# Gate and up products in float32r from exact 12-bit parts, and row additions by accumulating transfers, in a cross-attention and fp4 SwiGLU layer

## The chip, the cores and the metric

The kernel is written in Bass and Tile and runs on one core of a Trainium2 chip. The metric is the device time of one execution in microseconds (us). A core has four compute engines with one in-order instruction queue each, TensorE (PE), VectorE (DVE), ScalarE (ACT) and GpSimd (POOL), a fifth queue, SyncE (SP), that here issues nearly all transfers, 16 DMA engines that carry them out, the on-chip memory SBUF, and PSUM, where TensorE writes its results, in 8 banks of 128 x 512 float32 values.

## The reference

`x` is 8 batches x 512 rows x 256 columns in float32, the context 8 x 64 x 256. Cut to what matters, with `ln` for a layernorm without gamma and beta:

```python
y  = ln(x)
y  = ln(y + attention(y, y, y, causal=True)) * g1 + beta1
y  = ln(y + attention(y, ctx, ctx)) * g2 + beta2
ff = relu(y @ w1 + b1) @ w2 + b2              # 256 -> 1024 -> 256
x  = x + ln(y + ff) * g3 + beta3
q  = fp4(ln(x))                               # blocks of 16 values
h  = silu(q @ fp4(w_gate).T) * (q @ fp4(w_up).T)   # 256 -> 704
x  = x + fp4(h) @ fp4(w_down).T               # 704 -> 256
```

Attention has one head and no projections. `fp4` divides each block of 16 values by a sixth of its largest magnitude, rounds to the grid 0, 0.5, 1, 1.5, 2, 3, 4, 6 with the sign, and multiplies back.

## The kernel before

**Tiles.** Each batch is 4 row tiles (`NT`) of 128 rows (`P`). The width 256 is `ND` = 2 chunks of 128, the MLP's 1024 is `NF` = 8, the 704 (`I`) of gate and up is `NI` = 6 chunks, the last one 64 wide, and two halves (`HI`) of 352. Per batch there are five stages: self-attention (0), cross-attention (1), MLP (2), the gate/up products with silu (3) and the down product (4).

**Line numbers of the stages.** Transposes by TensorE stand at L419, the squares of a norm (ACT) at L488, its sums at L480 and L496, its power -1/2 on POOL at L503. `scaled_norm` has two VectorE steps per row tile, (r - mean) * g at L537 and r * rstd + beta at L545. `by_row` adds a row vector to four row tiles on VectorE (L557); it adds b2 to `r` and beta3 to `x`. `fp4` is L578 to L610: a reduction, two small steps on 44 block scales, three `scalar_tensor_tensor` or `tensor_tensor` steps of 704 columns with an Abs on ACT (L597) between them, and a last product (L610). Self-attention has its scores at L767, exp at L778 and values at L800. `turned` transposes either by products of TensorE, evicted by ACT (L831), or by transfers: ACT splits the values into planes of 16 bits (L843), SP's queue writes them to DRAM and reads them back transposed. Cross-attention is L883 (scores, laid into 128 rows of 256), L896 (ACT copies them out of PSUM), L900 (transposes), L927 (values). The MLP is L961 (first product), L969 (relu by ACT with b1 as bias), L981 (second product), L992 (VectorE adds it to `r`), L1003 and L1011 (norm and sum with `x`).

**Gate, up and down.** `zT` is the quantized, transposed input of the batch; `wgu` holds both quantized weights. For each row tile and each half of 352 columns, two float32 products (L1036), gate and up, go into a bank each. ACT takes silu of the gate bank into `h` (L1048), VectorE multiplies by the up bank (L1055). `h` is quantized, turned (planes by ACT at L1071 and two transfers, in the last batch by TensorE), multiplied by `wd` (L1116), added to `x` by VectorE (L1126) and stored by SP (L1133). A float32 product runs as two matmul instructions, so the 256 gate/up products are 512 instructions in the trace.

```python
plan.op("PE", ND * pe(HI), product, reads=[zT, ready["wgu"]], writes=[pair[j]],
        takes=[*pair, h])
```

**The order.** Nothing runs where the source puts it. Every step is a `plan.op`: engine, estimated cost, buffers read and written. `Plan.order` then lists all steps: each engine takes, of the steps whose inputs are there by the estimates and whose buffers are free, the one with the smallest key, the latest time at which it could start if the stages are to end at the times in `DUE` (a row for each batch, a column for each stage; `push` is added to the keys of the weights' steps). Steps are issued in that order, and each engine's queue keeps it on the chip. Buffers come in kinds with a fixed number (`x` 6, `z` 8, `hT` 8, `wide` 8 for `h` and its quantized magnitudes, and so on); buffers of an ordered kind can only be taken in the order in which the source creates them. At the head, the weights `w_gate`, `w_up` and `w_down` are quantized and turned by transfers into `wgu` and `wd`, beside the first batches.

Of the kernel before, what the change touches and what calls it, by code (L numbers as in the profile page):

```python
# [12 lines left out]
U16 = mybir.dt.uint16  # L13
AF = mybir.ActivationFunctionType
# [5 lines left out]
P = 128  # L20
# [11 lines left out]

PE_PASS = 0.429 / 512
# [5 lines left out]
TURN = 2.6  # L39
# [4 lines left out]
LOAD_EARLY = 2191.0  # L44
DUE = [
    [-1877.0, 638.0, 1236.0, -86.0, 359.0],
    [-498.0, 1140.0, 299.0, -53.0, 352.0],
    [251.0, 920.0, -109.0, 452.0, 665.0],
    [2244.0, 599.0, -92.0, 754.0, 95.0],
    [1032.0, 759.0, 1302.0, 1127.0, 22.0],  # L50
    [818.0, -579.0, 119.0, -1108.0, 586.0],
    [771.0, -1583.0, 341.0, 621.0, 85.0],
    [127.0, -388.0, -430.0, -94.0, -1479.0],
    [-2334.0],
# [6 lines left out]

def dve(cols):
    return 0.06 + cols * 1.06e-3
# [197 lines left out]
def kernel(  # L261
# [43 lines left out]
    def several(name, count, shape):  # L305
        return [fixed(f"{name}_{k}", shape) for k in range(count)]
# [3 lines left out]
    plan.kind("x", several("x", 6, [P, NT, D]))  # L310
# [3 lines left out]
    z_homes = several("z", 8, [P, D + 2])  # L314
    plan.kind("y0", y0_homes)
    plan.kind("z", z_homes)
    plan.kind("zT", several("zT", 6, [P, ND, SZ]))
# [3 lines left out]
    plan.share("zqT", "turned", 3)  # L321
    plan.kind("e", several("e", 1, [P, NT * (NT + 1) // 2 * P]))
    plan.kind("r", several("r", 3, [P, NT, D]))
    plan.kind("kq", several("kq", 4, [P, S // 2]))
    plan.kind("xp", several("xp", 6, [P, NT, SZ]))
    plan.kind("xpT", several("xpT", 3, [P, NT // 2 * P]))
# [3 lines left out]
    plan.kind("wide", several("h", 8, [P, NI * P]), ordered=False)  # L330
    plan.share("h", "wide", 5)
    plan.share("hm", "wide", 3)
    plan.share("wq", "wide", 7)
# [57 lines left out]
    c_rows = fixed("c_rows", [NF, P])  # L391
    b1_sb = fixed("cols", [P, NF])

    vecs = {}
    for name, v in (
        ("g1", g1), ("beta1", beta1), ("g2", g2), ("beta2", beta2), ("b2", b2),
        ("g3", g3), ("beta3", beta3),
    ):
        vecs[name] = (fixed(f"v_{name}", [P, D]), v)
    w1_sb = fixed("w1", [P, ND, DFF])  # L400
    w2_sb = fixed("w2", [P, NF, D])
    wgu = fixed("wgu", [P, ND, 2 * I])
    wd = fixed("wd", [P, NI, D])

    plan.kind("const", ["const"] * 13, ordered=False)
    ready = {}
    for name in ("cols", "g1", "beta1", "g2", "g3", "beta2", "beta3", "b2", "w1", "w2", "wgu", "wd", "pads"):
        ready[name] = plan.buf("const")
# [16 lines left out]
    def norm_stats(v, view, pairs):  # L425
# [18 lines left out]
        for ts_ in pairs:  # L444
            lo, hi = ts_[0], ts_[-1] + 1
            for t in ts_:
                plan.op(
                    "DVE", 0.33, lambda t=t: nc.vector.bn_stats(st(t), view(t)),
                    reads=[(v, t)], writes=[(s, ("st", t))],
                )  # L450
            plan.op(
                "DVE", 0.1 + 0.09 * len(ts_), lambda ts_=ts_: variances(ts_),
                reads=[(s, ("st", t)) for t in ts_],
                writes=[(s, ("var", lo))] + [(s, t) for t in ts_],
            )
            plan.op(
                "POOL", 1.05,
                lambda lo=lo, hi=hi: nc.gpsimd.tensor_tensor(
                    s.ap[:, 36 + lo : 36 + hi], s.ap[:, 32 + lo : 32 + hi], mhalf[:, lo:hi], ALU.pow
                ),  # L460
                reads=[(s, ("var", lo))], writes=[(s, ("rstd", t)) for t in ts_],
            )
            plan.op(
                "DVE", 0.15,
                lambda lo=lo, hi=hi: nc.vector.scalar_tensor_tensor(
                    s.ap[:, 40 + lo : 40 + hi],
                    s.ap[:, 24:32].rearrange("p (t k) -> p t k", k=2)[:, lo:hi, 0],
                    -1.0, s.ap[:, 36 + lo : 36 + hi], ALU.mult, ALU.mult,
                ),
                reads=[(s, ("rstd", t)) for t in ts_] + [(s, t) for t in ts_],  # L470
                writes=[(s, ("shift", t)) for t in ts_],
            )
        return s

    def sums_stats(v, view, s):
# [9 lines left out]
        for t in range(NT):  # L485
            plan.op(
                "ACT", 0.52,
# [43 lines left out]
    def scaled_norm(r, s, g, beta):  # L531

        sums_stats(r, lambda t: r.ap[:, t, :], s)
        for t in range(NT):
# [9 lines left out]
                "DVE", 0.4,  # L544
                lambda t=t: nc.vector.scalar_tensor_tensor(  # L545
                    r.ap[:, t, :], r.ap[:, t, :], s.ap[:, 36 + t : 37 + t], vecs[beta][0],
                    ALU.mult, ALU.add,
                ),
                reads=[(s, ("rstd", t)), ready[beta]], writes=[(r, t)],
            )  # L550

    def by_row(v, vec, f):

        for t in range(NT):
            plan.op(
                "DVE", dve(D),
                lambda t=t: nc.vector.tensor_tensor(  # L557
                    v.ap[:, t, :], v.ap[:, t, :], vecs[vec][0], f
                ),
                reads=[(v, t), ready[vec]], writes=[(v, t)],  # L560
            )
# [7 lines left out]
    def fp4(v, view, mkind, nblk):  # L569
# [18 lines left out]
        plan.op("DVE", 0.7, scales, reads=[q], writes=[q])  # L588
# [34 lines left out]

    def weights():
# [3 lines left out]
        plan.batch = 0  # L628
        for j, w in enumerate((w_gate, w_up)):
            for half, groups in enumerate(((0, 1), (2, 3, 4))):  # L630
# [23 lines left out]
                def apart(v=v, m=m, n=n, wide=wide):  # L654
                    k = halves(v.ap[:, :wide], D)
                    nc.scalar.copy(planes_of(m.ap[:, :wide], D), k)
                    if n > wide:
# [9 lines left out]
                )  # L667
                plan.op(
                    "SP", 1.8,
                    lambda d=d, g=g, j=j, groups=groups: nc.sync.dma_start_transpose(  # L670
                        wgu[:, :, ds(j * I + groups[0] * P, g * P)].bitcast(U16),
                        d.ap[:g].rearrange("g p h k -> (g p h) k"),
                    ),
                    reads=[d], writes=[(ready["wgu"], (j, half))], lag=TURN,
                )
                if not half:
# [9 lines left out]
                    def rest(d=d, j=j):  # L686
                        for c in range(ND):
                            nc.sync.dma_start_transpose(
                                wgu[:, c, ds(j * I + WI * P, RI)].bitcast(U16),
# [3 lines left out]
                    plan.op(  # L693
                        "SP", 1.2, rest, reads=[d], writes=[(ready["wgu"], (j, "rest"))], lag=TURN
                    )
# [28 lines left out]
    def columns():  # L724
        plan.batch = -1
        pt = plan.buf("bank")

        plan.op(
            "SP", 0.65, lambda: nc.sync.dma_start(c_rows, b1.rearrange("(c p) -> c p", p=P)),
            writes=[ready["cols"]],  # L730
        )
        plan.op(
            "PE", 0.2, lambda: nc.tensor.transpose(pt.ap[:, :NF], c_rows, ident[:NF, :NF]),
# [3 lines left out]
            "ACT", 0.2, lambda: nc.scalar.copy(b1_sb, pt.ap[:, :NF]),  # L737
            reads=[pt], writes=[ready["cols"]],
        )
        for name in ("g1", "beta1", "g2", "beta2", "b2", "g3", "beta3"):  # L740
# [4 lines left out]
            )  # L745

    def self_attention(b, xs):
# [13 lines left out]
        for k in range(NT):  # L761
# [3 lines left out]
            def scores(k=k, n=n, sc=sc):  # L765
# [11 lines left out]
                "ACT", act(n, True),  # L777
# [42 lines left out]
        scaled_norm(r, s, "g1", "beta1")  # L820
# [39 lines left out]
    def cross_attention(b, r, zs):  # L860
# [11 lines left out]
        )  # L872
        yT = turned(r, "yT", b < BY_PRODUCTS[1], lambda t: r.ap[:, t, :])
# [6 lines left out]
        def products():  # L880
            for c in range(ND):
                for i in range(2):
# [3 lines left out]
                    )  # L886

# [6 lines left out]
        plan.op("PE", 1.05, products, reads=[yT, zT], writes=[keys])  # L894
        kq = plan.buf("kq")
        plan.op("ACT", act(S // 2), lambda: nc.scalar.copy(kq.ap, keys.ap[:, : S // 2]), reads=[keys], writes=[kq])  # L896
# [48 lines left out]
        scaled_norm(r, s, "g2", "beta2")  # L945

    def mlp(b, r, xs):
# [5 lines left out]
        by_row(r, "b2", ALU.add)  # L953
        by_row(xs, "beta3", ALU.add)
        hT = []
        for f in range(NF):
            hp, h = plan.buf("bank"), plan.buf("hT")

            def product(f=f, hp=hp):
# [8 lines left out]
                "ACT", act(S, True),  # L968
# [3 lines left out]
                reads=[hp, ready["cols"]], writes=[h],  # L972
# [3 lines left out]
        for t in range(NT):  # L976
            fp = plan.buf("bank")

            def product(t=t, fp=fp):
# [11 lines left out]
                "DVE", 0.42,  # L991
# [27 lines left out]
    def glu(b, xs, s):  # L1019
# [7 lines left out]

        def gate_up(t):
            plan.stage = 3
            h = plan.buf("h")  # L1030
            for n in range(2):
                pair = [plan.buf("bank") for _ in range(2)]
                for j in range(2):
                    def product(t=t, n=n, j=j, gp=pair[j]):
                        for c in range(ND):
                            nc.tensor.matmul(  # L1036
                                gp.ap[:, :HI], zT.ap[:, c, ts(t, P)],
                                wgu[:, c, ds(j * I + n * HI, HI)],
                                start=(c == 0), stop=(c == ND - 1),
                            )  # L1040

                    plan.op(
                        "PE", ND * pe(HI), product, reads=[zT, ready["wgu"]], writes=[pair[j]],
                        takes=[*pair, h],
# [3 lines left out]
                    lambda n=n, h=h, gp=pair[0]: nc.scalar.activation(  # L1048
                        h.ap[:, ts(n, HI)], gp.ap[:, :HI], AF.Silu
                    ),  # L1050
                    reads=[pair[0]], writes=[(h, n)], table="silu",
                )
                plan.op(
                    "DVE", 0.45,
                    lambda n=n, h=h, gp=pair[1]: nc.vector.tensor_tensor(  # L1055
                        h.ap[:, ts(n, HI)], h.ap[:, ts(n, HI)], gp.ap[:, :HI], ALU.mult
                    ),
                    reads=[pair[1]], writes=[(h, n)],
# [52 lines left out]
        def last(t, hqT):  # L1111
            op = plan.buf("bank")

            def product(hqT=hqT, op=op):
                for c in range(NI):
# [8 lines left out]
            plan.op(  # L1124
                "DVE", 0.42,
                lambda t=t, op=op: nc.vector.tensor_tensor(  # L1126
                    xs.ap[:, t, :], op.ap[:, :D], xs.ap[:, t, :], ALU.add
                ),
                reads=[op], writes=[(xs, t)],
            )  # L1130
# [6 lines left out]

        if b == B - 1:
            hs = [gate_up(t) for t in range(NT)]
            for t in range(NT):  # L1140
                down(t, hs[t])
        else:
            for t in range(NT):
                down(t, gate_up(t))
# [18 lines left out]
    plan.push = 2035.0  # L1163
# [41 lines left out]
```

## Time and profile before

| | before |
|---|---|
| median of 3 runs (lowest to highest) | 575.76 us (575.72 to 576.1) |
| span of the profiled execution | 574.5 us |
| time of the profiled execution | its span; the runs' times lie 1.2 to 1.6 us above it |
| PE busy | 563.8 us, 98% |
| DVE busy | 447.8 us, 78% |
| ACT busy | 361.8 us, 63% |
| POOL busy | 62.2 us, 11% |
| gate/up products, L1036 | 512 instructions, 27% of the chain |
| down products, L1116 | 384 instructions, 15% of the chain |
| bytes moved by DMA | 66.88 MB, mean 116 GB/s |

The page is that of one execution, taken by the hardware profiler. "Busy" is the time in which an engine ran an instruction; "chain" is the chain of work that ended last, followed back from the last instruction, with its shares by engine and line. Groups of instructions are written line, engine, operation, output<-inputs, tile shape, count. The granted TensorE clock was full (1.000) through the whole span. Column names of a stage table are: start and end of the stage, its length, then busy time (instructions) of PE, PEld (the weight loads), DVE, ACT and POOL, mean granted clock, DMA share and GB/s.

### The profile page before, as it was taken

How to read it: one execution, taken by the hardware profiler on the slowest of the kernel's cores; microseconds unless marked ns; L12 is line 12 of the kernel's file. 1: busy time of each engine (PE TensorE's matmuls, PEld its weight loads, DVE VectorE, ACT ScalarE, POOL GpSimd, SP SyncE). 2: the span in 40 equal slices, each digit the busy share in tenths (PEclk: the TensorE clock that was granted, in tenths of full speed). 3: DMA queues.
4: the chain of work that ended last, by engine and by line, in shares of the span. 5: the costliest groups of instructions: out<-in, count | busy, mean ns of one | idle time of the engine just before them, and what ended most of it. 6: DMA issues, size and time to landing. Idle time of an engine off the chain costs nothing.

```text
span 574.5 us, 7037 instructions
## 1 busy us (share of the span) xinstructions
PE 563.8 (98%) x2209; PEld 391.2 (68%) x2209; DVE 447.8 (78%) x1125; ACT 361.8 (63%) x761; POOL 62.2 (11%) x93
## 2 busy tenths in 40 slices
PE   5999999999999999999999999999999999999997
PEld 2767584866747668658486667766765866877686
DVE  4789988869998865755259999978997656399892
ACT  4677869598887672791638558887845256364431
POOL 3521101011200120110101102210100000010000
PEclk9999999999999999999999999999999999999999
DMA  7770387246466513322023546585771421436501
GB/s 236 119 230 2 101 219 169 73 119 157 116 158 175 137 52 83 99 71 49 1 73 98 137 126 156 148 198 154 153 180 62 124 62 38 111 106 151 151 19 46
DMA packets 143220, 66.88 MB, mean 116 GB/s; under 512 B 107976, under 2 KB 142672, under 8 KB 143184
## 3 DMA queue, kind: packets, MB, share of 16 engines
q1 hardware_dynamic: 143184, 66.44, 45.4%
q8 instruction: 17, 0.28, 0.2%
q14 instruction: 19, 0.16, 0.1%
HBM read 10.42 MB, written 29.66 MB: 70 GB/s over the span
## 4 chain that ended last, share of the span: by engine, by line
PE 98%; ACT 1%; DMA 0%; SPq 0%; issue 0%; DVE 0%; ACTq 0%
PE bank L1036 27%; PE bank L981 19%; PE bank L961 19%; PE bank L1116 15%; PE bank L767 7%; PE bank L800 6%; PE bank L419 2%; PE bank L927 1%; PE bank L883 1%; DMA z<-in_ctx_dram 0%; ACT squares L488 0%; PE bank L900 0%; SPq L358 0%; ACT turned L831 0%; PE bank L1102 0%
## 5 line engine op out<-in xcount | busy, mean ns | idle before, releaser
L1036 PE MATMUL bank<-wgu,turned 128*128 128x352 f32 x512 | 157.5, 460 | 0.0
L1036 PEld LDWEIGHTS bank<-wgu,turned 128*128 128x128 f32 x512 | 96.3, 190 | 51.8 <-issue 1.7
L981 PE MATMUL bank<-w,hT 128*128 128x256 f32 x512 | 112.6, 379 | 0.0
L961 PE MATMUL bank<-turned,w 128*128 128x512 f32 x256 | 112.5, 593 | 0.0
L981 PEld LDWEIGHTS bank<-w,hT 128*128 128x128 f32 x512 | 97.0, 190 | 13.8
L1116 PE MATMUL bank<-wd,hqT 128*128 128x256 f32 x384 | 87.2, 380 | 0.0
L961 PEld LDWEIGHTS bank<-turned,w 128*128 128x128 f32 x256 | 48.2, 190 | 56.9 <-issue 51.7
L1116 PEld LDWEIGHTS bank<-wd,hqT 128*128 128x128 f32 x384 | 72.4, 190 | 14.2 <-issue 2.9
L503 POOL TENSOR_TENSOR ln<-ln,mhalf 128x4 f32<-128x4 f32 x32 | 37.7, 1180 | 352.0 <-DVE ln L496 352.0
L603 DVE SCALAR_TENSOR_TENSOR h<-h,h 128x704 f32<-128x704 f32 (+2 forms) x76 | 66.8, 883 | 3.8 <-ACT h L597 3.4
L488 ACT ACTIVATE squares<-r,ln 128x256 f32<-128x256 f32 x96 | 48.7, 508 | 32.0 <-DVE ln L480 29.7
L969 ACT ACTIVATE hT<-bank,cols 128x512 f32<-128x512 f32 x64 | 42.8, 681 | 21.7 <-PE bank L961 21.5
L1048 ACT ACTIVATE h<-bank 128x352 f32<-128x352 f32 x64 | 29.2, 460 | 36.4 <-PE bank L1036 32.5
L1071 ACT COPY h<-h 128x1408 uint16<-128x1408 uint16 x28 | 38.0, 1362 | 19.4 <-DVE h L610 17.9
L1055 DVE TENSOR_TENSOR h<-h,bank 128x352 f32<-128x352 f32 x64 | 32.4, 516 | 12.3 <-PE bank L1036 8.6
L992 DVE SCALAR_TENSOR_TENSOR r<-bank,r 128x256 f32<-128x256 f32 x32 | 13.5, 421 | 35.0 <-PE bank L981 34.7
L767 PE MATMUL bank<-turned 128*128 128x512 f32 (+3 forms) x128 | 39.8, 457 | 0.4 <-ACT turned L831 0.4
L597 ACT ACTIVATE h<-h 128x704 f32<-128x704 f32 (+2 forms) x38 | 29.7, 788 | 14.0 <-DVE h L591 13.9
L800 PE MATMUL bank<-y,e 128*128 128x258 f32 x160 | 36.8, 381 | 0.0
L800 PEld LDWEIGHTS bank<-y,e 128*128 128x128 f32 x160 | 30.1, 190 | 5.9 <-issue 1.0
L591 DVE SCALAR_TENSOR_TENSOR h<-h,q 128x704 f32<-128x704 f32 (+2 forms) x38 | 33.5, 883 | 0.2
L610 DVE TENSOR_TENSOR h<-h,q 128x704 f32<-128x704 f32 (+2 forms) x38 | 33.4, 879 | 0.2
(90 smaller groups left out, 639.9 us busy)
## 6 DMA issues: line engine op xcount, KB each, us to landing
zd<-zm SPq DMA_DIRECT2D x25, 512.0 KB, 3.0
hd<-h SPq DMA_DIRECT2D x30, 352.0 KB, 3.0
out_dram<-x SPq DMA_DIRECT2D x32, 128.0 KB, 1.7
x<-in_x_dram SPq DMA_DIRECT2D x7, 512.0 KB, 5.3
w<-in_L_xattn_w_dram SPq DMA_DIRECT2D x2, 1024.0 KB, 7.4
z<-in_ctx_dram SPq DMA_DIRECT2D x16, 64.0 KB, 4.6
zd<-h SPq DMA_DIRECT2D x2, 384.0 KB, 3.1
h<-in_L_ffn_w_down_dram SPq DMA_DIRECT2D x2, 352.0 KB, 4.2
```

Of the source, the lines that this page charges most:

```text
L488: lambda t=t: nc.scalar.activation(squares, view(t), AF.Square, bias=s.ap[:, 24 + t : 25 + t], accum_out=s.ap[:, 28 + t : 29 + t],),
L503: lambda: nc.gpsimd.tensor_tensor(s.ap[:, 36:40], s.ap[:, 32:36], mhalf, ALU.pow),
L591: lambda: nc.vector.scalar_tensor_tensor(blocks_of(view()), blocks_of(view()), TIE, each(rc()), ALU.mult, ALU.mult),
L603: lambda reverse=reverse, f=f: nc.vector.scalar_tensor_tensor(view(), mm(), LEAST, view(), ALU.max, f, reverse1=reverse),
L767: nc.tensor.matmul(sc.ap[:, :n], yT.ap[:, c, ts(k, P)], yT.ap[:, c, k * P :], start=(c == 0), stop=(c == ND - 1),)
L800: nc.tensor.matmul(av.ap[:, : D + 2], e.ap[:, ds(start[k] + (t - k) * P, P)], y0.ap[:, k, :], start=(k == 0), stop=(k == t),)
L961: nc.tensor.matmul(hp.ap, w1_sb[:, c, ts(f, P)], yT.ap[:, c, :], start=(c == 0), stop=(c == ND - 1),)
L969: lambda f=f, hp=hp, h=h: nc.scalar.activation(h.ap, hp.ap, AF.Relu, bias=b1_sb[:, f : f + 1]),
L981: nc.tensor.matmul(fp.ap[:, :D], hT[f].ap[:, ts(t, P)], w2_sb[:, f, :], start=(f == 0), stop=(f == NF - 1),)
L1036: nc.tensor.matmul(gp.ap[:, :HI], zT.ap[:, c, ts(t, P)], wgu[:, c, ds(j * I + n * HI, HI)], start=(c == 0), stop=(c == ND - 1),)
L1071: lambda: nc.scalar.copy(planes(), h.ap[:, :I].bitcast(U16).rearrange("p (k h) -> p h k", h=2)),
L1116: nc.tensor.matmul(op.ap[:, :D], hqT.ap[:, ts(c, P)], wd[:, c, :], start=(c == 0), stop=(c == NI - 1),)
```

## The change

**Gate and up.** Each operand is split into exact parts of 12 bits in float32r, a 32-bit type in which a product is one matmul instruction of the built program (a float32 product is two). `high` is the operand times 1 - 2^-13, rounded by writing it as float32r (ACT), `low` the rest (DVE), and `diff` is high - 4096 low (DVE). The weights get the same parts, with `low` scaled by 4096. In batches 0 to 5 three products per half and weight are made: high x high and low x low' into one bank (`a`), diff x diff into another (`d`). ACT copies `d`, scaled, into SBUF, VectorE adds `a`, and the silu and the multiplication apply a common scale. From batch 6 on (`WHOLE_FROM`) all four products of high and low go into one bank, as before the change followed by one silu and one multiplication; the low weights are rescaled by ACT between batches 5 and 6.

**Row additions.** `add_row` adds a row vector by a transfer that accumulates into SBUF, issued by POOL. beta1 goes into the context rows (the values of cross-attention, whose weights add up to 1) and, through an added column of its score product, into a bias of the copy of the scores; beta2 goes into the MLP's bias by `hidden_columns` and, summed with b2 in DRAM, into `r`; beta3 into `x`. The second step of `scaled_norm` becomes an ACT copy with a scale. The residual addition of down becomes an ACT copy into an `o` tile, of which there is one, and an accumulating transfer by POOL, except in the last batch.

**The plan.** Buffer counts go down to make room (`x` 5, `z` 4, `zT` 4, `kq` 1, `xp` 2, `xpT` 2, `wide` 6), estimated costs are set anew, and `DUE` and `push` have new values.

Lines of the changed kernel that the text names: L584 `add_row`, L1077, L1085 and L1097 the MLP, L1148 the rescaling, L1172 the four products, L1210 the three products, L1226 and L1233 copy of `d` and addition of `a`, L1308 down, L1319 VectorE's addition of the last batch, L1327 and L1332 copy into `o` and its transfer.

```diff
+WHOLE_FROM = 6
+CUT = 1.0 - 2.0**-13
+PART = 2.0**12
+FROM_B = -1.0 / (PART + 1.0)
+WHOLE = 1.0 + 1.0 / PART
...
+    for part in ("high", "low", "diff"):
+        plan.kind(part, several(part, 1, [P, ND, S], F32R))
...
+    plan.kind("up", several("up", 2, [P, HI]), ordered=False)
+    plan.kind("o", several("o", 1, [P, D]))
...
+    def add_row(v, view, row, shape, reads=()):
+        plan.op(
+            "POOL", 1.2,
+            lambda: nc.gpsimd.dma_start(
+                view(), row.partition_broadcast(P).unsqueeze(1).to_broadcast(shape),
+                accum_op=ALU.add,
+            ),
+            reads=list(reads), writes=[v], lag=3.0,
+        )
...
+    def parts(v, cols, out, reads, writes, scaled=False):
+        high, low = out[:2]
+        plan.op(
+            "ACT", act(cols),
+            lambda: nc.scalar.activation(high(), v(), AF.Copy, scale=CUT),
...
+        def rest():
+            nc.vector.tensor_tensor(low(), v(), high().bitcast(F32), ALU.subtract)
+            if len(out) > 2:
+                nc.vector.scalar_tensor_tensor(
+                    out[2](), low().bitcast(F32), -PART, high().bitcast(F32), ALU.mult, ALU.add
+                )
+            if scaled:
+                nc.vector.tensor_scalar(low(), low().bitcast(F32), PART, None, ALU.mult)
...
-        by_row(r, "b2", ALU.add)
-        by_row(xs, "beta3", ALU.add)
+        add_row(r, lambda: r.ap, row, [P, NT, D], [ready["row"]])
+        add_row(xs, lambda: xs.ap, beta3, [P, NT, D])
...
+                    a, d = plan.buf("bank"), plan.buf("bank")
+                    def product(t=t, these=these, a=a, d=d):
+                        for to, ks in ((a, (0, 1)), (d, (2,))):
+                            for k in ks:
+                                for c in range(ND):
+                                    nc.tensor.matmul(
+                                        to.ap[:, :HI], cut[k].ap[:, c, ts(t, P)],
+                                        wgu[k][:, c, these],
...
+                    plan.op(
+                        "ACT", act(HI),
+                        lambda view=view, d=d: nc.scalar.activation(
+                            view(), d.ap[:, :HI], AF.Copy, scale=FROM_B
+                        ),
...
+                    plan.op(
+                        "DVE", dve(HI),
+                        lambda view=view, a=a: nc.vector.tensor_tensor(
+                            view(), a.ap[:, :HI], view(), ALU.add
+                        ),
...
+            if b == B - 1:
+                plan.op(
+                    "DVE", 0.335,
...
+            else:
+                o = plan.buf("o")
+                plan.op(
+                    "ACT", act(D), lambda op=op, o=o: nc.scalar.copy(o.ap, op.ap[:, :D]),
+                    reads=[op], writes=[o],
+                )
+                plan.op(
+                    "POOL", 1.0,
+                    lambda t=t, o=o: nc.gpsimd.dma_start(
+                        xs.ap[:, t, :], o.ap, accum_op=ALU.add
+                    ),
+                    reads=[o], writes=[(xs, t)], lag=2.2,
+                )
```

## The prediction

> **What bounds the kernel now.** I read the page's busy shares and its chain first, then busy times by stage, then the chain in order of time.
>
> ```profile
> span 574.5 us, 7037 instructions
> PE 563.8 (98%) x2209; PEld 391.2 (68%) x2209; DVE 447.8 (78%) x1125; ACT 361.8 (63%) x761; POOL 62.2 (11%) x93
> ...
> PE 98%; ACT 1%; DMA 0%; SPq 0%; issue 0%; DVE 0%; ACTq 0%
> ```
>
> TensorE sets the time from beginning to end: 98% of the chain. The stages (start:end, length, then busy time of each engine) show where it does not:
>
> ```profile
> 0.00:50.00 50.00, 42.44 (x197) 29.38 (x198) 36.83 (x153) 30.14 (x83) 17.33 (x42) 1.00 0.64 168
> 50.00:497.15 447.15, 447.15 (x1708) 305.67 (x1706) 351.17 (x862) 300.07 (x613) 42.08 (x49) 1.00 0.45 114
> 497.15:561.58 64.43, 64.43 (x258) 47.81 (x258) 58.07 (x107) 29.89 (x59) 2.76 (x2) 1.00 0.40 105
> 561.58:574.50 12.92, 9.80 (x51) 8.32 (x50) 1.70 (x5) 1.71 (x6) 0.00 (x0) 0.99 0.15 51
> ```
>
> PE is idle for 7.6 us in the first 50 and 3.1 us at the end, and nowhere else. I cut the rest at two events: 497.15 is the end of the last MLP's second product, which I call M, and 561.58 is the end of VectorE's last fp4 step, E. Between them VectorE has 58.1 us of work in 64.4 us: it is nearly level with PE in this last stage. Prices of PE come from the chain (start, length, matmuls):
>
> ```profile
> 483.33 13.81 PE bank L981 x64
> ...
> 531.62 18.93 PE bank L1036 x64
> 550.55 5.18 PE bank L1116 x24
> ```
>
> So one gate/up instruction of 352 columns takes 18.93/64 = 0.296 us, one of 256 columns 0.216, one down (12 instructions) 2.59. A float32 product is two such instructions. VectorE's prices are read from start to start in the timeline near the end:
>
> ```profile
> 551.63 0.95 DVE L1055 TENSOR_TENSOR h<-h,bank 128x352 f32<-128x352 f32 x2
> 552.63 0.89 DVE L603 SCALAR_TENSOR_TENSOR h<-h,h 128x704 f32<-128x704 f32 x1
> 553.44 0.88 DVE L578 TENSOR_REDUCE q<-h 128x44 f32<-128x704 f32 x1
> 554.24 0.88 DVE L603 SCALAR_TENSOR_TENSOR h<-h,h 128x704 f32<-128x704 f32 x1
> 555.04 0.18 DVE L585 TENSOR_SCALAR q<-q 128x44 f32<-128x44 f32 x1
> 555.25 0.43 DVE L586 RECIPROCAL q<-q 128x44 f32<-128x44 f32 x1
> 555.60 0.83 DVE L610 TENSOR_TENSOR h<-h,q 128x704 f32<-128x704 f32 x1
> ```
>
> A 704-wide step takes 0.80, the two small ones 0.21 and 0.35, a 352-wide one 0.43: fp4 of one h is 5 x 0.80 + 0.56 = 4.55 us.
>
> **PE's part.** The 512 gate/up instructions (151.4 us) go. 832 float32r ones come: 576 in three passes (batches 0 to 5) and 256 in four. No row shows one. Upper bound: 0.296, what half a float32 product takes now. Lower: a quarter of a float32 product, 0.148, as operands in two parts make four part products. I take 0.148, since the diff multiplies single parts; then 832 x 0.148 = 123.1, a saving of 28.3. Weight loads could spoil this, as 832 replace 512:
>
> ```profile
> 34.73 0.58 PE L419 MATMUL bank<-ident,z 64*128 64x64 f32 x6
> ```
>
> Six small products, each with a load of 128 columns, start within 0.58 - 0.27 (the last one's length) = 0.31 us, one per 0.062. A load is thus at most 0.062 and lies under a 0.148 product. The Trainium skill, "TensorE: Matmul & The Clock Gate", LDWEIGHTS, gives a load as columns/1.2 in ns, 107 ns here, and its Part 3 lets a load overlap running matmuls only in another row group; by that the change would add 832 x 0.107 = 89 us, and the row speaks against it. Added: 32 one-column products with beta1 and 16 with beta2, two instructions each at up to 0.062: 5.8 us. PE's sum is 563.8 - 28.3 + 5.8 = 541.3 us. If PE stayed the bound, that would be the whole story.
>
> **VectorE and ScalarE.** VectorE loses 64 scalings with beta (L545, 25 us), 64 row additions (L557, 21) and 28 of 32 residual additions (9). It gains 96 PSUM additions (42), parts of zT (17) and of the weights (8.5), 1.3 of small steps: +13 net. ScalarE gains 96 PSUM copies at 0.36 (35), 64 scalings (28), parts (8 + 3), 28 copies of the down result (7) and a rescaling of the low weights, 2.4: +83. In total both stay below PE; in the head the built order has no more VectorE work than before. What matters is where the order puts it.
>
> **Up to M.** I counted the built instruction order of the changed kernel. Before its M stand 450 of the 832 part products, 102 of 192 down products (before: 384 of 512 instructions, 114 of 192) and all small ones. PE's busy time up to M was 497.15 - 7.56 = 489.6; now 489.6 - 113.6 + 66.6 - 12 x 2 x 0.216 + 5.8 = 443.2. With the same 7.6 idle, M is at 450.8. New waits come on top. ScalarE copies each down result into one o tile and POOL adds it by a transfer; the next copy waits for that transfer, and behind it in ScalarE's queue stand PSUM evictions that free PE's banks; behind POOL's wait stand the pow steps of other batches' norms. The row additions into r (issued by POOL) must land before L992's successor; some 13 us of MLP products cover them. Batch 3's stretch has 51.7 us of VectorE for 51.2 of PE. Bounds: 0 (up to here PE waited nowhere after 50 us) to 15 (two drifts of 10 and 9 us, by which VectorE's work outgrows PE's, minus bank slack). I take 4: M at 454.8.
>
> **M to E: VectorE sets it.** Behind M the order still holds 13 tiles of gate/up (8 before). VectorE's queue from M to E: 14 fp4 of h (63.8), one of zq (6.3), 48 steps of 352 (20.9), 8 part steps of 512 at 0.6 (4.8), 8 of 256 at 0.4 (3.2), small 0.4: 99.4 us, where it was 56.4. PE has 98.5 - 23.3 = 75.2 us there. So the stage takes at least 99.4. It took 64.4 for 56.4 of work before, 8 us of waits; fewer now for PE, more for ScalarE's Abs between two fp4 steps (0.75 us at 558.63). I take 5, bounds 2 to 12: E at 454.8 + 104.4 = 559.2.
>
> **E to the end: the single o tile.** The copies into o must go in creation order. Batch 4's last down stands behind all gate/up products of batch 7, so the eight downs of batches 5 and 6, finished in five held banks and later, queue behind it: nine copies, each waiting for the transfer before. The last six stand in ScalarE's queue behind the last eviction of h's transpose, some 7 us after E (two downs of 2.59 and evictions between). One round c is copy + issue + landing.
>
> ```profile
> L896 ACT COPY kq<-bank 128x256 f32<-128x256 f32 x8 | 2.9, 366 | 15.1 <-PE bank L883 15.1
> ```
>
> ```profile
> out_dram<-x SPq DMA_DIRECT2D x32, 128.0 KB, 1.7
> ...
> x<-in_x_dram SPq DMA_DIRECT2D x4, 128.0 KB, 2.1
> ...
> v_g<-in_L_xattn_g_dram SPq DMA_DIRECT2D x3, 128.0 KB, 4.9
> ```
>
> No row has an adding transfer issued by POOL. Lower: 0.37 + 0.43 (issue of v_g on SP's queue) + 1.7 = 2.5; upper: 0.37 + 1.18 (a POOL pow) + 4.9 = 6.5. I take 0.37 + 0.8 + 2.1 = 3.3, nearest to the 2.1: same size, queues nearly empty by then. Tail: 7 + 6 x 3.3 + 2.2 (last store) = 29.0 (24 to 48), against 12.9 before. "DMA: Bandwidth & Descriptors", Anatomy of one DMA, fits 2.0 us + bytes/436e3, 2.3 us for this transfer; by it c is about 2.7 and the tail 25. No run here yet shows whether VectorE holds up POOL's descriptors, as "SBUF — State Buffer", SBUF: two separate sides, warns.
>
> **Sum.** 559.2 + 29.0 = 588.2 us of span; the median lies 575.76 - 574.5 = 1.26 above the span: 589.5 us. PE's 22 us are saved and lost twice: to VectorE's queue behind M and to the o chain.
>
> **Rivals.** *PE remains the bound up to its last gate/up product* and VectorE's queue behind M hides: PE's sum without the 23.3 us (eight downs, 24 transposes) behind that product is 518.0, at 525.6 with the idle 7.6; then three downs (7.8), nine rounds and a store: 7.8 + 29.7 + 2.2 = 39.7, 566.6 with the 1.26. Faster. For it: PE waited nowhere in the trace; against: 99.4 us of counted VectorE work. It decides once M to E falls below about 88 us with M at 454.8. *The rounds block ScalarE throughout*: c of 5 and more makes the tail 39, and 19 earlier rounds and 24 row additions hold evictions by some 10 us: 610. For it: one tile, in-order queues; against: ScalarE has slack. *A part product is no quarter*: at 0.296 PE gains 832 x 0.148 = 123 us, about 690. For it: no row here has a float32r product; against: a float32 product runs as two instructions of 0.296, four part products in all, and the diff's operands are single parts.
>
> **Chances.** Main 0.70, PE bound 0.10, ScalarE blocked 0.17, slow part products 0.03. The main case's own roots (M -4/+11, waits -3/+7, tail -5/+19, taken as independent) give 582 to 612. The range 573 to 611 takes in the blocked case and leaves out the PE-bound case, the slow products and the far ends of the main case, 0.2 together. The main case reaches below 576 only where M, waits and tail all lie at their lower ends and the VectorE prices too: 0.04 of it, split evenly over faster and same. A change under 0.2% cannot be told from none here: faster 0.12, same 0.02, slower 0.86.
>
> **What would show it.** Right: L1210 at about 0.149 us from start to start; M near 455; from M VectorE without gaps and PE with them; nine copies L1327 in the last 35 us, 3.3 us apart, with PE idle. Wrong: a chain of PE to the end, a span below 573, or part products of 0.19 or more.

## The result

The changed kernel takes 714.71 us (median of 4 runs, 712.34 to 716.54), against 575.74 before (the median with a fourth run of it): a ratio of 1.242 (95% interval 1.239 to 1.245). The direction was forecast, the size was not: 589.5 us with a range of 573 to 611. Times of kernels are medians of undisturbed runs; in the last experiment one run of four, 1.6% above the fastest, is left out.

The page of the changed kernel: its span, the busy shares, and the chain.

```profile
span 711.1 us, 8247 instructions
PE 597.5 (84%) x2625; PEld 454.8 (64%) x2625; DVE 464.5 (65%) x1120; ACT 440.7 (62%) x968; POOL 117.7 (17%) x143
PE 39%; issue 21%; DMA 18%; ACT 9%; DVE 6%; SPq 3%; POOL 2%; POOLq 0%; DVEq 0%; ACTq 0%
```

No engine is full any more, transfers carry 18% of a chain that had 0% of them, and TensorE is busy for longer (597.5 us, from 563.8) though the prediction had it at 541.3. The four stages of the prediction, cut again at the end of the last MLP product (M, now 557.38) and of the last fp4 step (E, now 680.35); columns as before:

```profile
0.00:50.00 50.00, 37.24 (x165) 26.79 (x165) 23.21 (x95) 23.93 (x59) 19.52 (x40) 0.90 0.84 171
50.00:557.38 507.38, 446.48 (x1875) 326.31 (x1876) 336.21 (x841) 350.20 (x783) 84.86 (x88) 0.93 0.56 115
557.38:680.35 122.97, 99.29 (x515) 89.72 (x514) 103.41 (x180) 61.27 (x112) 6.99 (x8) 0.89 0.35 81
680.35:711.10 30.75, 14.51 (x74) 11.98 (x72) 1.70 (x4) 5.31 (x16) 6.35 (x8) 0.80 0.39 87
```

TensorE is idle for 12.8 us of the first 50 (7.6 before) and for 60.9 us of the next stage, in which it waited nowhere before. The granted clock, 1.00 before (0.99 in the last stage), is 0.90, 0.93, 0.89 and 0.80.

What ended TensorE's waits, in the waits view (total us, times, longest), those on turned tiles alone:

```profile
PE bank L1077 <- DMA turned<-zd: 15.4, 4, 4.7
PE bank L865 <- DMA turned<-zd: 14.0, 2, 7.8
PE bank L1308 <- DMA hqT<-hd: 10.4, 5, 5.3
PE bank L982 <- DMA turned<-zd: 9.1, 2, 8.3
```

Together 48.9 us; the same view of the kernel before has no such line. One place in the chain (start, length):

```profile
292.03 9.86 DMA zd<-zm
...
301.95 4.87 DMA turned<-zd
...
306.95 3.75 PE bank L865 x4
```

The write of the planes took 9.86 us, with a median of 3.3 over all 25. Beside it ran an addition of beta3 to `x`, issued at 290.23, and from 294.61 on a residual addition of 128 KB. The issues view (KB of each, median us to landing) of the changed kernel:

```profile
zd<-zm SPq DMA_DIRECT2D x25, 512.0 KB, 3.3
x<-in_L_xattn_beta_dram POOLq DMA_DIRECT2D x8, 512.0 KB, 10.2
r<-row_d POOLq DMA_DIRECT2D x8, 512.0 KB, 11.1
x<-o POOLq DMA_DIRECT2D x28, 128.0 KB, 2.7
```

The additions to `r` and `x` take three times as long as the write of the planes, a plain transfer of the same size. It is no accident where those to `r` fall: the addition waits until the planes of `r` are copied, and so does the write of these planes. In the timeline of SP and of POOL they stand 0.28 us apart:

```profile
509.08 0.39 SPq L947 DMA_DIRECT2D zd<-zm  x1
```

```profile
509.36 1.30 POOL L584 DMA_DIRECT2D r<-row_d  x1 [3.25 <-ACT zm L941]
```

Six of the eight additions to `r` are issued within 0.3 us of such a write; the transposing read behind it lands after 12.1 to 12.6 us in the three cases where the trace tells it, against 4.2 to 5.7 us away from them. In the trace no instruction waits for a row addition itself; what TensorE waits for are the transfers beside it.

### The profile page after: what moved, and what is told of

It reads as the page before. It is cut to its first block, busy times and chain, and to the rows that moved or that the text cites. A ratio compares the mean times of both kernels' runs of the same rounds, so it can differ in the third digit from the quotient of the medians.

```text
span 711.1 us, 8247 instructions
## 1 busy us (share of the span) xinstructions
PE 597.5 (84%) x2625; PEld 454.8 (64%) x2625; DVE 464.5 (65%) x1120; ACT 440.7 (62%) x968; POOL 117.7 (17%) x143
## 4 chain that ended last, share of the span: by engine, by line
PE 39%; issue 21%; DMA 18%; ACT 9%; DVE 6%; SPq 3%; POOL 2%; POOLq 0%; DVEq 0%; ACTq 0%
PE bank L1077 9%; PE bank L1097 8%; PE bank L1210 7%; DMA turned<-zd 7%; PE bank L1308 5%; PE bank L898 4%; DMA zd<-zm 3%; PE bank L865 3%; DMA w<-in_L_xattn_w_dram 3%; ACT zm L941 2%; DMA zd<-h 2%; POOL x L1332 1%; ACT squares L517 1%; DMA x<-in_x_dram 1%; DMA hqT<-hd 1%
## 5 line engine op out<-in xcount | busy, mean ns | idle before, releaser
L1077 PE MATMUL bank<-turned,w 128*128 128x512 f32 x256 | 121.6, 623 | 16.4 <-DMA turned<-zd 15.4
L1097 PE MATMUL bank<-w,hT 128*128 128x256 f32 x512 | 118.3, 389 | 3.0 <-ACT h L1226 2.4
L1097 PEld LDWEIGHTS bank<-w,hT 128*128 128x128 f32 x512 | 99.2, 196 | 19.3 <-ACT h L1226 2.7
L1308 PE MATMUL bank<-wd,hqT 128*128 128x256 f32 x384 | 93.1, 398 | 10.9 <-DMA hqT<-hd 10.4
L1077 PEld LDWEIGHTS bank<-turned,w 128*128 128x128 f32 x256 | 49.0, 198 | 70.8 <-issue 57.4
L1308 PEld LDWEIGHTS bank<-wd,hqT 128*128 128x128 f32 x384 | 76.0, 201 | 24.5 <-issue 9.3
L1210 PE MATMUL bank<-wgu_high,high 128*128 128x352 f32 x192 | 57.9, 383 | 7.2 <-ACT h L1226 3.9
L1332 POOL DMA_DIRECT2D x<-o x28 | 24.4, 870 | 209.1 <-ACT o L1327 206.9
L1085 ACT ACTIVATE hT<-bank,b 128x512 f32<-128x512 f32 x64 | 42.6, 686 | 16.2 <-PE bank L1077 15.9
L1263 ACT COPY h<-h 128x1408 uint16<-128x1408 uint16 x28 | 38.1, 1362 | 19.9 <-DVE h L638 10.9
L1210 PE MATMUL bank<-wgu_low,low 128*128 128x352 f32 x192 | 48.3, 333 | 1.0 <-DVE low L662 1.0
L1210 PE MATMUL bank<-wgu_diff,diff 128*128 128x352 f32 x192 | 48.7, 335 | 0.6 <-ACT h L1226 0.3
L865 PEld LDWEIGHTS bank<-turned 128*128 128x128 f32 x128 | 26.5, 223 | 33.7 <-issue 20.6
L1210 PEld LDWEIGHTS bank<-wgu_high,high 128*128 128x128 f32 x192 | 34.7, 195 | 17.1 <-ACT h L1226 4.9
L606 DVE TENSOR_REDUCE q<-h 128x44 f32<-128x704 f32 (+2 forms) x38 | 33.4, 880 | 9.4 <-DMA h<-in_L_ffn_w_up_dram 6.2
L1210 PEld LDWEIGHTS bank<-wgu_diff,diff 128*128 128x128 f32 x192 | 34.6, 195 | 1.8 <-ACT h L1226 0.6
## 6 DMA issues: line engine op xcount, KB each, us to landing
x<-in_L_xattn_beta_dram POOLq DMA_DIRECT2D x8, 512.0 KB, 10.2
```

The costliest lines, as they stand in the source:

```text
L606: lambda: nc.vector.tensor_reduce(amax(), blocks_of(view()), AX.X, ALU.max, apply_absolute_value=True),
L865: nc.tensor.matmul(sc.ap[:, :n], yT.ap[:, c, ts(k, P)], yT.ap[:, c, k * P :], start=(c == 0), stop=(c == ND - 1),)
L1077: nc.tensor.matmul(hp.ap, w1_sb[:, c, ts(f, P)], yT.ap[:, c, :], start=(c == 0), stop=(c == ND - 1),)
L1085: lambda f=f, hp=hp, h=h: nc.scalar.activation(h.ap, hp.ap, AF.Relu, bias=b1_sb[:, f : f + 1]),
L1097: nc.tensor.matmul(fp.ap[:, :D], hT[f].ap[:, ts(t, P)], w2_sb[:, f, :], start=(f == 0), stop=(f == NF - 1),)
L1210: nc.tensor.matmul(to.ap[:, :HI], cut[k].ap[:, c, ts(t, P)], wgu[k][:, c, these], start=(k == ks[0] and c == 0), stop=(k == ks[-1] and c = ...
```

## The experiments

Theory A: the 512 KB row additions hold up the turning transfers for which TensorE waits. Rivals: B, the one `o` tile or the products' added steps on ScalarE and VectorE; C, the order that the new due times give.

**Bytes of the row additions.** Places in the queues are unchanged; all 24 row additions, the 8 of 128 KB to the context too, write one partition.

```diff
-                view(), row.partition_broadcast(P).unsqueeze(1).to_broadcast(shape),
+                view()[:1], row.partition_broadcast(1).unsqueeze(1).to_broadcast([1, *shape[1:]]),
```

> The changed kernel in its own order, but each of the 24 row additions writes one partition instead of 128 (left out: the additions on the other 127). Every instruction, wait and queue place stays, only the bytes go. Theory A (the row additions, 10 to 12 us each, are issued with the turning transfers and slow them from about 3 + 4.5 us to as much as 10 + 12; TensorE waits for the turned tiles): the waits on turned tiles, some 45 us of TensorE's 92 us of gaps, go, and with them part of the lower clock: 635 to 660 us. Theory B (the one o tile: ScalarE's and SyncE's queues stand behind its transfers): 695 to 715. Theory C (the order and VectorE's and ScalarE's added work set the time, whatever the transfers take): 690 to 715.

Measured: 649.13 us, ratio to before 1.128 (1.125 to 1.130): 66 us less. M moves from 557.4 to 490.0, by 67.4 us; the two stages behind it change by 3 us at most. In the views of this run, the row additions are short and the waits on turned tiles nearly gone:

```profile
x<-in_L_xattn_beta_dram POOLq DMA_DIRECT2D x8, 4.0 KB, 2.2
r<-row_d POOLq DMA_DIRECT2D x8, 4.0 KB, 3.2
```

```profile
PE bank L1077 <- DMA turned<-zd: 3.2, 1, 3.2
PE bank L1308 <- DMA hqT<-hd: 2.0, 2, 1.3
```

48.9 us of waits became 5.2, and TensorE's busy time fell by 21.8 us (to 575.7) though its instructions are the same ones in the same order. The lower clock behind the waits fits this: the time at half clock fell by 56.6 us, of which half is lost where TensorE is at work. A holds for about half of the loss.

**Two `o` tiles in turn**, same order.

```diff
-    plan.kind("o", several("o", 1, [P, D]))
+    plan.kind("o", ["o"])
+    o_ring = several("o", 2, [P, D])
...
+                at = o_ring[(b * NT + t) % 2]
```

> The changed kernel in its own order, with two o tiles taken in turn, so that a copy waits only for the transfer before the last. Theory A: only the tail after the last fp4 step gets shorter, from 34 us to some 20 to 25: 700 to 706 us. Theory B: also the stretch up to the last MLP product, by 20 us and more: below 690. Theory C: the tail alone, as A.

705.19 us, 1.225 (1.222 to 1.228). The tail fell from 30.8 to 25.3 us; M came 4 us earlier. The rounds of the o tile cost little before M in this order, against what B expected (20 us and more); what one tile costs against none, a later run asks.

**Both of these edits.**

> Both edits, in the same order (row additions on one partition only, two o tiles). Theory A: the sum of the two, 620 to 650 us. Theory B: 650 to 690, all of it there with the two o tiles alone. Theory C: 680 to 705.

641.0 us, 1.113 (1.112 to 1.115): nearly the sum of the two, 639.6.

**Row additions alone, in the kernel before.**

```diff
-        by_row(r, "b2", ALU.add)
-        by_row(xs, "beta3", ALU.add)
+        add_row(r, lambda: r.ap, b2, [P, NT, D])
+        add_row(xs, lambda: xs.ap, beta3, [P, NT, D])
...
```

> The kernel before with one part of the change alone: b2 is added to r and beta3 to x by 16 accumulating transfers issued by POOL, in place of 64 additions on VectorE (21 us of its work gone). The planner places the steps anew, with the due times of before. Theory A: each transfer falls on a turning transfer, and TensorE, which waited nowhere, now waits: 595 to 625 us. Theories B and C: 570 to 580 us, as VectorE only loses work.

638.62 us, 1.110 (1.106 to 1.113), above the range I gave A. Sixteen transfers that take 20 us of work off VectorE cost 63 us, with no float32r and no `o` tile in the program. The planner placed the steps anew, and TensorE's order is not that of before, so part of the 63 may be the order. TensorE's waits on turned tiles are 33.7 us of it, and its busy time is 18.4 us longer (582.2). The longest of these waits is this piece of the chain:

```profile
461.80 16.90 DMA turned<-zd
...
478.83 5.83 PE bank L972 x8
```

**Gate/up alone**, with row and residual additions by VectorE and the change's due times.

```diff
-        add_row(r, lambda: r.ap, row, [P, NT, D], [ready["row"]])
-        add_row(xs, lambda: xs.ap, beta3, [P, NT, D])
+        by_row(r, "v_row", v_row)
+        by_row(xs, "v_beta3", v_beta3)
...
```

> The gate/up part of the change alone, as nearly as the memory allows: the additions to r and x are made by VectorE (64 of 256 columns), the residual additions too (no o tile); the 8 small additions to the context stay transfers. The planner places the steps anew with the due times of the change. Theory A (the 512 KB row additions collide with the turning transfers): what is left is the 641 us of the run with one-partition additions and two o tiles, less the tail of about 15 us, plus some of VectorE's 31 us added: 620 to 650. Theory B (the products themselves, with their banks, copies and additions, cost most): 660 and more.

632.21 us, 1.098 (1.096 to 1.100), inside A's range. Without any of the large transfers, 57 us of loss stay. Whether the products or the order make it, this run can't tell.

**The same bytes, issued later.**

```diff
-        add_row(r, lambda: r.ap, row, [P, NT, D], [ready["row"]])
-        add_row(xs, lambda: xs.ap, beta3, [P, NT, D])
+        add_row(r, lambda: r.ap, row, [P, NT, D], [ready["row"], yT])
+        add_row(xs, lambda: xs.ap, beta3, [P, NT, D], [r])
```

> The changed kernel with all its bytes, but the addition to r also waits for the turned tile to land, and the addition to x for the one to r: the same transfers at another time. The planner places the steps anew. Theory A as a collision in time: most of the 66 us that the bytes cost comes back, 650 to 680 us. Theory A' (the bytes cost the same wherever they stand, for instance by slowing engines or all later transfers): 700 to 720.

688.65 us, 1.194 (1.191 to 1.197): 26 us came back, between the two expectations; the planner placed the steps anew here too. TensorE's waits on the turns of `r`, `y` and `z` went from 38.5 to 20.2 us, those on the turns of `h`, which start at other times, from 10.4 to 28.4:

```profile
PE bank L1308 <- DMA hqT<-hd: 28.4, 8, 8.1
```

With 25 + 28 turns through DRAM in the kernel, one for each 13 us, most places for a 10 us transfer lie beside one.

**Other due times** (and pushes), nothing else; they were chosen because the planner's list then ends earlier.

> The changed kernel with other due times and pushes alone, chosen so that the planner's own list, by its estimates, ends earlier; no instruction differs, only places in the queues. Theory C (the order is what costs): 620 to 660 us. Theory A (the bytes cost 66 us in any order, and the one o tile a tail): 680 to 720.

662.02 us, 1.149 (1.146 to 1.152): 53 us less from the order alone, just above the range of C and below that of A. The two causes overlap: another order also moves the collisions.

**Without large transfers and `o` tile, rows folded into VectorE's steps, other due times** (and a planner's estimate of 0.162 us for a part product).

```diff
-        scaled_norm(r, s, "g2")
+        scaled_norm(r, s, "g2", v_row)
...
-            lambda: nc.vector.tensor_tensor(b1_sb, cols[:, :NF], pt.ap[:, :NF], ALU.add),
+            lambda: nc.vector.tensor_tensor(b1_sb, cols[:, :NF], pt.ap[:, :NF], ALU.subtract),
...
```

With `v_row` the second step of the norm is r * rstd + (b2 + beta2) on VectorE.

> A version without the 512 KB transfers and without the o tile: b2 + beta2 enters in the second step of the norm on VectorE (hidden bias b1 - w1.T b2), beta3 is added to x by one VectorE step of 1024 columns per batch, residual additions by VectorE, gate/up as in the change, other due times. TensorE's work: 563.8 of before, less 151.4 of gate/up, plus 832 x 0.162 = 134.8, plus some 5 us = 552 us; with before's idle 10.7 us and a little more: 570 to 590 us if nothing else holds TensorE up (theories A and C together); above 610 if the products' added steps on ScalarE and VectorE hold it up (theory B).

588.92 us, 1.024 (1.020 to 1.028). Its page:

```profile
PE 562.7 (95%) x2625; PEld 437.7 (74%) x2625; DVE 487.2 (82%) x1188; ACT 425.3 (72%) x912; POOL 71.9 (12%) x99
```

TensorE's busy time is that of the kernel before (563.8). From start to start, waits taken out, its gate/up instructions take 101.1 us (576 in three passes) and 41.8 us (256 in four), 142.9 in all, against 152.4 before: a gain of 9.5 us. 5.7 us of it go to the added column products, also from start to start; what is left fits the clock (17.1 us at half), and idle time grew from 10.7 to 28.4 us.

**Gate/up alone with other due times.**

> The run with the gate/up part alone (632 us), with other due times and pushes and nothing else; the planner's list ends earlier by its own estimates. Theory C (what is left of the loss there is the order that the change's due times give): 580 to 600 us, near the 589 of the folded version. Theory B (the products' copies and additions hold TensorE up in any order): 615 to 632.

591.15 us, 1.027 (1.025 to 1.029): 41 of the 57 us that stayed in the gate/up run were the order. Theory C holds for these. The folded version lies only 2 us lower, with due times of its own.

**Residual additions by VectorE**, row additions still by transfers.

```diff
-            if b == B - 1:
-                plan.op(
-                    "DVE", 0.335,
...
-            else:
-                o = plan.buf("o")
...
+            plan.op(
+                "DVE", 0.335,
+                lambda t=t, op=op: nc.vector.tensor_tensor(
+                    xs.ap[:, t, :], op.ap[:, :D], xs.ap[:, t, :], ALU.add
+                ),
...
```

> The changed kernel with the residual additions of batches 0 to 6 made by VectorE again (no o tile, no copy, no transfer of 128 KB); the row additions stay transfers. The planner places the steps anew. If the one o tile costs its tail alone: 34 us of tail become some 15, VectorE gets 9 us more: 690 to 705. If its rounds hold up ScalarE and SyncE before the last MLP product too: below 680.

687.41 us, 1.196 (1.193 to 1.199): 27 us less than the change, between the two expectations. The planner placed the steps anew, so part of it may be the order.

**Row transfers that don't add.**

```diff
-                accum_op=ALU.add,
+                accum_op=ALU.add if shape[1] == 1 else ALU.bypass,
```

> The changed kernel with every instruction in the same place, but the 16 row transfers to r and x write the row without adding (left out: the addition; the 8 to the context still add). Same bytes written, nothing read back from the tile. If adding is what makes them long: they land in 5 to 6 us, as the plain 512 KB loads of x do, and 30 to 45 of the 66 us come back, 670 to 685 us. If the bytes or the issue by POOL are: still 9 us and more, 700 to 715.

696.75 us, 1.210 (1.204 to 1.215). 18 us came back, which puts the time between the two expectations, 3 us below the second. The transfers still take 9.0 (`x`) and 10.2 us (`r`): the addition is not what makes them long. POOL's issues are as short here as in the one-partition run (POOL is busy for 108.4 us in both, 117.7 in the changed kernel), so shorter issues explain at most these 18 of its 66 us.

**Only the additions to `r` on one partition.** The new last argument is the number of partitions.

```diff
-        add_row(r, lambda: r.ap, row, [P, NT, D], [ready["row"]])
+        add_row(r, lambda: r.ap, row, [P, NT, D], [ready["row"]], 1)
```

> The changed kernel with every instruction in the same place, but the 8 additions to r write one partition instead of 128 (left out: the other 127); those to x and to the context are whole. Each addition to r starts within 0.3 us of the write of a turning transfer, those to x seldom do. If the collision is what costs: 40 to 50 of the 66 us come back, 662 to 675. If each 512 KB costs the same wherever it falls: 8 of 16, some 30 us, 680 to 690.

664.9 us, 1.155 (1.149 to 1.161): 50 of the 66 us, from half of the large transfers. Where a transfer falls counts for more than how many there are.

## Why the prediction was wrong, step by step

The direction was right for part of the forecast's reasons only. Against the kernel before, M to E became 58.5 us longer and the tail 17.8, where 40 and 16 were forecast; but M, forecast 42 us earlier, came 60.2 us later.

| term | predicted | measured | difference |
|---|---|---|---|
| M | 454.8 | 557.4 | +102.6 |
| M to E | 104.4 | 123.0 | +18.6 |
| E to the end | 29.0 | 30.8 | +1.8 |
| median above span | 1.26 | 3.6 | +2.3 |
| sum | 589.5 | 714.7 | +125.3 |

**The step that failed** is M, at this sentence: the row additions "must land before L992's successor; some 13 us of MLP products cover them". It asks only who reads `r` next. It put no price on the landing, and did not ask what else uses the DMA engines in those microseconds. The readers of `r` were covered; TensorE's wait for the transfers beside it was not in the sum at all, and the bounds of 0 to 15 us left it out. On one partition the same additions give M = 490.0, so 67.4 of the 102.6 us go with their bytes. The kernel's source held the answer: `mlp` turns `r` in the line above `add_row`, and both transfers are released by the same copy of the planes.

Of the other 35.2 us, 18.1 are idle time (29.7 us up to M in the one-partition run, 11.6 assumed) and 17.2 are busy time (460.4 us, 443.2 assumed). The busy part has two roots. A part product is 0.162 us from start to start (median), not 0.148. The stretches in the chain of waits show it (3.86/24 = 0.161):

```profile
161.55 3.86 PE bank L1210 x24
169.09 3.88 PE bank L1210 x24
```

For the 450 products ahead of M that is 6.3 us. Most of the remaining 10.9 us fits the clock, which I took to stay full: up to M the one-partition run spends 17.1 us at half clock (a mean of 0.98), which costs at most 8.5. In the trace's clock record the changed kernel spends 118.1 us of its span at 0.5, the one-partition run 61.5, the kernel before 0.3. Behind the longest wait a part product takes 0.29 us (609.71 to 610.00 in the timeline) for some microseconds:

```profile
609.25 0.66 PE L1172 MATMUL bank<-wgu_high,high 128*128 128x352 f32 x1 [15.61 <-ACT high L657]
609.71 0.50 PE L1172 MATMUL bank<-wgu_low,high 128*128 128x352 f32 x1
610.00 0.50 PE L1172 MATMUL bank<-wgu_high,high 128*128 128x352 f32 x1
```

The Trainium skill, "TensorE: Matmul & The Clock Gate", Part 1, says that the clock is halved after an idle window of about 3.4 us and comes back after a busy one. The record agrees in length and place: its 16 stretches at 0.5 last 3.41 us or multiples of it, but for the last, which the end of the kernel cuts off. In the last 3.41 us of each of the 15 TensorE is busy for 86% or more. In the 3.41 us before a stretch it is busy for between 0 and 76%, so not every one of these windows was idle as a whole. A wait thus costs more than its length, and a prediction that adds a wait to a TensorE that had none owes this term.

**M to E: the mechanism held up to 600 us, and its waits were mis-sized.** VectorE is busy for 103.4 us there. (99.4 were counted at prices from start to start, which come out lower: in the kernel before they give 56.4 where the profile has 58.1 busy.) Of waits I took 5 us, at most 12; they are 19.6. The stage in three pieces:

```profile
557.38:600.00 42.62, 31.43 (x151) 26.49 (x149) 40.92 (x82) 27.29 (x62) 5.74 (x6) 0.88 0.20 43
600.00:625.00 25.00, 14.58 (x62) 12.76 (x63) 16.29 (x28) 13.87 (x17) 0.00 (x0) 0.66 0.80 181
625.00:680.35 55.35, 53.29 (x304) 50.47 (x303) 46.21 (x72) 20.11 (x33) 1.25 (x2) 1.00 0.26 65
```

In the first piece VectorE is full, as forecast. In the second, batch 6 goes over to four passes. TensorE waits for 15.6 us there, up to 609.25 (the line at 609.25 above), for the parts of batch 6's input, and VectorE then for its first products, made in part at half clock, 6.4 us of the 9.2 in this line:

```profile
DVE h L1190 <- PE bank L1172: 9.2, 7, 4.3
```

Ahead of these parts stand VectorE's last step on that input (from 596.51), its turn through DRAM (write 599.96, read 602.92) and, in ScalarE's queue, the rescaling of the low weights (606.14 to 608.67). I had counted the rescaling as 2.4 us of ScalarE and not asked what is queued behind it; whether it or the turn held the parts longer, the trace doesn't tell. In the third piece TensorE is the fuller engine: it has 99.3 us of work between M and E, where I had counted 75.2 and left it out as the lesser. No run tests these shares.

**E to the end: right, by its own steps.** Nine copies in the last 36 us. The last six begin 7.5 us after E (7 predicted) and are 3.4 us apart (3.3 predicted): a copy of 0.37, 0.3 until the issue, and 2.65 from the issue's start to the landing, the issue's 0.85 included. The forecast's 0.8 and 2.1 for the last two, 2.9 together, come close to their 2.95 by another split. The fit in the Trainium skill, "DMA: Bandwidth & Descriptors", Anatomy of one DMA, gives an estimate of 2.3 us for such a transfer, the trace 2.6 to 2.7, so the row decides. By the same fit the estimate for the 512 KB of a row addition is 3.2 us; measured, 10 to 11.

**The rivals.** That TensorE stays the bound up to its last gate/up product fell. The slow part products (about 690 us) came nearest to the time, by accident: a part product is 0.162 us, and the two-tile and one-partition runs show other causes. The blocked ScalarE came out small in the given order: 9.5 us with two tiles, 5.4 of them in the tail. Without the o tile's copies and transfers it is 27 us, with the steps placed anew.

**TensorE's saving** was sized at 28.3 us and is 9.5 in the folded version. At full clock, a half of gate or up takes 6 x 0.162 = 0.97 us in three passes and 8 x 0.162 = 1.30 in four; in float32 it took 4 x 0.296 = 1.18. The four-pass batches lose.

**Sums and readings.** The 8 us of VectorE's waits in the kernel before are 6.4 by the busy time of its own row. 96 column products at 0.062 us are 6.0 us, not 5.8, and PE's work behind M is 541.3 - 443.2 = 98.1, not 98.5. None of this decides anything.

**What the order is worth.** With the due times of the change, gate/up alone takes 632 us, with others 591. I used the built order to count what stands where, and priced it with before's idle time; I never asked whether it keeps TensorE supplied. Causes overlap, so the shares are no sum: 66 us for the bytes in the given order, 53 for the order with the bytes, 41 for the order without them.

No version here beats the kernel before; the best is 2.4% slower. Whether a still better order would make the float32r products pay stays open, and so do why a row that is repeated over 128 partitions takes 10 us and by what it holds up the transfers beside it.

## What to carry to other kernels

A step that is moved to a transfer leaves the engine but joins every transfer that is released by the same event: look up in the diff what else starts when it starts, and price the wait of the bound engine for that neighbour, not only that of the step's own reader. A TensorE that never waited loses twice when it begins to, by the wait and by the clock behind it. And a fitted order is part of the kernel: when pieces and due times change together, price the order by itself, with the pieces left as they are.

## What was not expected of the hardware

A transfer issued by POOL that lays one row over 128 x 4 rows of 256 columns (512 KB) lands after 10 to 11 us, and without adding after 9 to 10; with one partition (4 KB) it takes 2.2 to 3.2 us. While it runs, plain turning transfers of 3.0 and 4.5 us take as much as 10 and 13. A float32r pass of 352 columns takes 0.162 us at full clock, where half of a float32 instruction (0.296) would be 0.148.
